# A graph layer on one core: the scan, the moved VectorE steps and the edge look-up of its first two parts rewritten

## The chip, the cores and the metric

The kernel runs on one core of one Trainium2 chip. The metric is the device time of one execution in microseconds (us). TensorE is called PE in the profile, its weight load PEld, VectorE is DVE, ScalarE is ACT, GpSimd is POOL and SyncE is SP. Each engine works through its own queue of instructions in the order in which they were built into the program.

## The reference

The layer has 6250 nodes with 256 features and 206,250 edges, each a pair (src, dst). A node is normalised to `xn`. Three things are then computed and added.

```
h  = xn @ W                          # 64 features a node
el = h @ Wl.T ; er = h @ Wr.T        # 4 heads a node
e  = exp(leaky_relu(el[src] + er[dst], 0.2))
w  = e / max(segment_sum(e, src), 1e-12)[src]
gnn = elu(segment_sum(w[:, head] * h[dst], src) + b)      # 4 heads x 64
x1 = x + gnn + linear_attention(xn)  # keys' softmax runs over all nodes
x2 = x1 + moe(layernorm(x1))         # 8 experts, top 2, 256 -> 256 -> 256
```

## The kernel before, in words

Nodes are cut into 49 tiles of 128 rows. The kernel has three stages.

**First part.** `project` takes the nodes in groups of 4 tiles. For each tile it normalises the rows (`xn`, L310, DVE), transposes and multiplies them by one joined weight matrix (L316, L321, PE), and ACT copies the queries, the keys with values (`kv`) and the table row (`tab`, L328) out of PSUM. DVE copies the four `el` columns (L329) and keeps a running maximum of the keys (`kmax`, L335). The table goes to DRAM; the edge stage gathers from it.

Between the groups run the 51 calls of `sort_batch`, three after each group and the last twelve after all of them. A batch is 32 columns of 128 edges. DVE builds a one-hot `ob` of each edge's block of nodes (L365). PE counts each column (L371) and DVE turns the counts into running sums (the scan, L375) and subtracts the column's own count (`before`, L380). `ahead` (L390) spreads that for a matmul. PE adds the rank within the column (`tri`, L398) and `ahead` (L399). ACT copies the result to f16, and DVE multiplies by `ob` (L410), sums over the 26 blocks (L413), doubles the rank (`rank2`, L415) and compares it with a row of numbers (`ohp`, L422). PE then places the edges with it (L428). `context` runs beside the last twelve batches: it takes the maximum off the keys (L468, DVE), exponentiates (L469, ACT) and multiplies keys by values (L472, PE).

**Edge stage.** `pack(q)` makes the edge list for the two node tiles 2q and 2q+1. It counts with two matmuls (`here` L830, `total` L832) and a scan (L833), goes through `to_i` (L846 to L848) to the one-hots `ohc`, `rc` and `ohp` in seven rounds (L858, L865, L870, DVE), and sums them into `s_ps` (L875, PE). From `s_i` (L880) come the gather's indices `dst_x` (L886). Then POOL issues the gathers: 35 for each tile (L906), in five buffers `xe` of seven gathers each; eight such buffers exist. `pack(q+1)` is called in the middle of tile 2q.

For each tile `look` fetches `el` of the edges' own nodes. It builds one-hots `oh` (L919), transposes them in two halves (L932) and multiplies them with `elw` (L939). The result stands in PSUM once for each of 12 column groups, 4 quarters and 3 bf16 parts. DVE sums the three parts into `er` (L943), once for each half. At the start of the tile `weights` puts the quarters' columns in place and adds them up (L960 to L964), then adds the gathered `xe` of the five buffers one after the other (L967), and forms `z` (L969), the exponential and `bank` (L972). `sums` multiplies the one-hots by the weights (`ohw`, L980, DVE) and sums the gathered rows (`a_ps`, L987, PE).

**Between the steps of the edge stage** the function `some_more` issues the next step of other work: first `attention`, and then for each block of 4 finished node tiles `finish_steps`: `front` (L640 to L675), `route` (L692 to L723) and the experts, `hidden` (`h_ps`, L731) and `result`. `result` puts one `y_ps` (L747) for each tile and expert, which DVE adds to `x` (L751). The last experts run after the last tile.

The order on each engine is not the order of the source. A scheduler places every instruction when the program is built, by its own costs, so a change in one step can move others.

Of the kernel before, what the change touches and what calls it, by code (L numbers as in the profile page):

```python
# [35 lines left out]
def tile_gps_layer(  # L36
# [173 lines left out]

    tri = sp.tile([P, P], F16, name="tri")
    nc.vector.tensor_scalar(tri, iota_f, piota, None, op0=OP.is_gt)
    delta = sp.tile([NB, NB], F16, name="delta")
    nc.vector.tensor_scalar(delta, iota_f[:NB, :NB], piota[:NB], None, op0=OP.is_equal)

    starts = sp.tile([NB, BW // CB, CB], F32, name="starts")
    nc.vector.memset(starts, 1.0)
    nc.vector.memset(starts[:, :, 0:1], 0.0)

# [68 lines left out]
    def project(t0, n):  # L288
# [15 lines left out]
        nc.vector.tensor_scalar_mul(rn[:, :n], rn[:, :n], float(D) ** 0.5)  # L304
        tab = qw.tile([P, GT, TW], F32, name="tab")
        nc.gpsimd.memset(tab[:, :, TW - 1:TW], 1.0)  # L306
        for j in range(n):
            t = t0 + j
            xn = qw.tile([P, D], F32, name="xn")
            nc.vector.tensor_scalar(  # L310
                xn, xt[:, j, :], stats[:, t, 0:1], rstd[:, t:t + 1],
                op0=OP.subtract, op1=OP.mult,
            )
            xT_ps = mps.tile([P, DC, P], F32, name="tp")
            for c in range(DC):
                nc.tensor.transpose(xT_ps[:, c, :], xn[:, c * P:(c + 1) * P], ident)  # L316
            xT = qw.tile([P, DC, P], F32, name="xT")
            nc.scalar.copy(xT, xT_ps)
            pr = mps.tile([P, PW], F32, name="pr")
            for c in range(DC):  # L320
                nc.tensor.matmul(  # L321
                    pr, lhsT=xT[:, c, :], rhs=wcat[:, c, :], start=(c == 0), stop=(c == DC - 1)
                )
            nc.scalar.activation(q_all[:, t, :], pr[:, :HID], AF.Copy, scale=rn[:, j:j + 1])
            nc.scalar.activation(
                kv[:, t, :2 * HID], pr[:, HID:3 * HID], AF.Copy, scale=rn[:, j:j + 1]
            )
            nc.scalar.copy(tab[:, j, :TW - 1], pr[:, O_TAB:O_EL])  # L328
            nc.vector.tensor_copy(el[:, t, :], pr[:, O_EL:PW])  # L329
            rows = P if t < NT - 1 else last  # L330
            k_t = kv[:rows, t, :HID]
            if t == 0:
                nc.vector.tensor_copy(kmax, k_t)
            else:
                nc.vector.tensor_max(kmax[:rows], kmax[:rows], k_t)  # L335
        nc.sync.dma_start(
            out=table[t0 * P:(t0 + n) * P, :].rearrange("(t p) f -> p t f", p=P),
            in_=tab[:, :n, :],
        )
# [8 lines left out]
    def sort_batch(t):  # L348
# [19 lines left out]
        )  # L368
        n_ps = sps.tile([NB, BW], F32, name="n_ps")
        for c in range(w):  # L370
            nc.tensor.matmul(  # L371
                n_ps[:, c:c + 1], lhsT=ob[:, c, :], rhs=ones16[:, 0:1], start=True, stop=True
            )
        inc = sw.tile([NB, BW], F32, name="inc")
        nc.vector.tensor_tensor_scan(  # L375
            inc[:, :w], flat(starts)[:, :w], n_ps[:, :w], 0.0,
            op0=OP.mult, op1=OP.add,
        )
        before = sw.tile([NB, BW, 2], F16, name="before")
        nc.vector.tensor_tensor(  # L380
            before[:, :w], inc[:, :w, None].to_broadcast([NB, w, 2]),
            n_ps[:, :w, None].to_broadcast([NB, w, 2]), op=OP.subtract,
        )
        if w == BW:
            nc.scalar.copy(ntot[:, bs], inc[:NQ].rearrange("q (b c) -> q b c", c=CB)[:, :, CB - 1])
        else:
            for b, e in enumerate(ends):
                nc.scalar.copy(ntot[:, bs][:, b:b + 1], inc[:NQ, e - 1:e])
        ahead = sw.tile([NB, BW, NB], F16, name="ahead", bufs=1)
        nc.vector.tensor_tensor(  # L390
            pairs(ahead[:, :w]), two(before[:, :w], NB // 2), row(delta, NB // 2), op=OP.mult
        )
        r_ps = sps.tile([P, BW // BB, 512], F32, name="r_ps")
        r16 = sw.tile([P, BW, NB], F16, name="r16", bufs=1)
        for i, a in enumerate(range(0, w, BB)):
            z = min(w, a + BB)
            part = r_ps[:, i, :(z - a) * NB]
            nc.tensor.matmul(part, lhsT=tri, rhs=flat(ob[:, a:z]), start=True, stop=False)  # L398
            nc.tensor.matmul(  # L399
                part, lhsT=ones16[:NB, :], rhs=flat(ahead[:, a:z]), start=False, stop=True  # L400
            )
# [8 lines left out]
        nc.vector.tensor_tensor(flat(r16[:, :w]), flat(r16[:, :w]), flat(ob[:, :w]), op=OP.mult)  # L410
        rank = sw.tile([P, BW], F16, name="rank")
        with nc.allow_low_precision("one summand of each sum is not zero"):
            nc.vector.tensor_reduce(rank[:, :w], r16[:, :w], axis=AX.X, op=OP.add)  # L413
        rank2 = sw.tile([P, BW, 2], F16, name="rank2")
        nc.vector.tensor_copy(rank2[:, :w], rank[:, :w, None].to_broadcast([P, w, 2]))  # L415
        rv = sw.tile([P, BW, 2, NB], F16, name="rv")
# [23 lines left out]

    def context():
        km_ps = mps.tile([HID, P], F32, name="tp")
        nc.tensor.transpose(km_ps, kmax, ident)
# [371 lines left out]
    def pack(q):  # L815
# [8 lines left out]
        for u in range(U):  # L824
# [5 lines left out]
            nc.tensor.matmul(flat(here), lhsT=upto, rhs=flat(ohs), start=True, stop=True)  # L830
            total = pe.tile([P, S, NBT], F32, name="e_ps")
            nc.tensor.matmul(flat(total), lhsT=ones16, rhs=flat(ohs), start=True, stop=True)  # L832
# [82 lines left out]
    def look(b, k):  # L915

        if k == 0:
# [6 lines left out]
            )  # L924
            seen[b] = oh, gw.tile([P, GC, S, H], F32, name="er")
        elif k < 3:
            oh, er = seen[b]
            gh = GC // 2
# [14 lines left out]
            nc.vector.tensor_reduce(  # L943
                er[:, g0:g0 + gh].rearrange("p g s h -> p (g s) h"),
                e_ps.rearrange("p g s i h -> p (g s) h i"), axis=AX.X, op=OP.add,
            )

    def weights(xes, er):
        z = gw.tile([P, CW, H], F32, name="z")

        def of(q0, n, a, m):

            zq = z[:, q0 * CS:(q0 + n) * CS].rearrange("p (s j) h -> p s j h", j=CS)
            return zq[:, :, a:a + m]

        def er_of(q0, n, a, m):
            return er[:, a:a + m, q0:q0 + n].rearrange("p g s h -> p s g h")

        more = GC - 1 - CS
        nc.vector.tensor_copy(of(0, S, 0, CS), er_of(0, S, 1, CS))  # L960
        nc.vector.tensor_copy(z[:, CPT - more:CPT], er[:, GC - more:, S - 1])
        head, tail = of(1, S - 1, 0, more), of(0, S - 1, CS - 1, 1)
        nc.vector.tensor_add(head, head, er_of(0, S - 1, GC - more, more))
        nc.vector.tensor_add(tail, tail, er_of(1, S - 1, 0, 1))  # L964
        for k, xe in enumerate(xes):
            zk = z[:, k * EB:(k + 1) * EB]
            nc.vector.tensor_add(zk, zk, xe[:, :, :H])  # L967
# [210 lines left out]
```

## Time and profile before

| | |
|---|---|
| median of 17 runs | 3153.06 us (3148.53 to 3166.56) |
| profiled execution | 3159.26 us, span of its instructions 3157.5 us |
| mean granted clock of TensorE | 0.782 of full speed |
| busy: PE, PEld, DVE, ACT, POOL | 2163.7, 1642.1, 2040.3, 681.9, 1753.9 us |
| first gather starts | 492.82 us |
| gathers | 1715 (L906), mean 1016 ns |

In a timeline or chain row the first number is the start in us from the span's start and the second the length in us; a bracket holds the idle time of the engine before it and what ended it, as far as the profile could infer. In a row of a group "busy us, mean ns | idle before" follow the shapes. A row of windows gives, for one stretch of time, each engine's busy time.

### The profile page before, as it was taken

Reading aid. Unit: us, or ns where it says so; the run is one execution under the profiler, and the core shown is the slowest. Engines: PE = TensorE matmul, PEld = TensorE weight load, DVE = VectorE, ACT = ScalarE, POOL = GpSimd, SP = SyncE. Lnnn points to the kernel's source line nnn. Section 1 sums busy time; section 2 is a strip of 40 time slices with the busy share of each in tenths; the row PEclk is TensorE's granted clock in tenths of the full one; section 3 lists DMA queues with packets and bytes.
Section 4 is the critical chain, followed back from the end, with each engine's and each line's share of the span. In section 5 each row is a group of like instructions: output and inputs, shape, how many; then the busy total and the mean of one; then the engine's idle time right before and its main releaser. Section 6 shows DMA issues by size and latency. Waiting matters only on the chain. (4 is left out here: it accounts for less than half of the span.)

```text
span 3157.5 us, 40348 instructions
## 1 busy us (share of the span) xinstructions
PE 2163.7 (69%) x15298; PEld 1642.1 (52%) x15298; DVE 2040.3 (65%) x4719; ACT 681.9 (22%) x1365; POOL 1753.9 (56%) x1753
## 2 busy tenths in 40 slices
PE   6777763454545487768877778587685885848868
PEld 3444442344444365646665566456564564646645
DVE  8888886476667547655764685556755666556733
ACT  3333320111221122122222121121120211212123
POOL 1000005777777565578666575775766757757520
PEclk8777665766667688879887888688796887968879
DMA  2000201132222311121111111211112112111110
GB/s 63 27 26 20 20 1 33 24 66 53 54 51 39 89 25 33 21 41 23 36 29 33 29 33 23 40 27 29 33 26 38 27 28 33 29 30 31 28 15 9
DMA packets 106684, 103.98 MB, mean 33 GB/s; under 512 B 42726, under 2 KB 78788, under 8 KB 106484
## 3 DMA queue, kind: packets, MB, share of 16 engines
q0 software_dynamic: 54880, 60.70, 13.5%
q1 hardware_dynamic: 49908, 39.75, 4.5%
q8 instruction: 122, 2.00, 0.3%
q10 hardware_dynamic: 1696, 0.89, 0.1%
q14 instruction: 78, 0.64, 0.1%
HBM read 86.57 MB, written 14.65 MB: 32 GB/s over the span
## 5 line engine op out<-in xcount | busy, mean ns | idle before, releaser
L906 POOL DMA_INDIRECT xe<-table,dst_x x1715 | 1742.5, 1016 | 982.2 <-issue 486.5
L987 PE MATMUL a_ps<-ohw,xe 128*65 128x128 f32 x4410 | 619.5, 301 | 52.1 <-DVE ohw L980 51.9
L987 PEld LDWEIGHTS a_ps<-ohw,xe 128*65 128x65 f32 x4410 | 574.6, 156 | 95.5 <-DVE ohw L980 74.1
L747 PE MATMUL y_ps<-w2s,hT 128*128 128x256 f32 x1568 | 414.8, 406 | 105.5 <-DVE x L751 90.9
L747 PEld LDWEIGHTS y_ps<-w2s,hT 128*128 128x128 f32 x1568 | 307.4, 204 | 211.6 <-DVE x L751 103.2
L731 PE MATMUL h_ps<-tokT,w1s 128*128 128x512 f32 (+2 forms) x896 | 401.4, 565 | 7.1 <-ACT hT L739 5.7
L967 DVE TENSOR_TENSOR z<-z,xe 128x28 f32<-128x28 f32 x245 | 40.9, 188 | 551.8 <-DMA xe<-table,dst_x 537.8
L980 DVE TENSOR_TENSOR ohw<-oh,bank 128x1280 f32<-128x1280 bf16 x196 | 322.6, 1650 | 110.7 <-PE a_ps L987 109.8
L875 PE MATMUL s_ps<-rc,ohp 128*128 128x144 f16 x2525 | 240.7, 264 | 178.3 <-DVE rc L865 157.3
L751 DVE SCALAR_TENSOR_TENSOR x<-y_ps,comb,x 128x256 f32<-128x256 f32 x392 | 187.0, 481 | 240.4 <-PE y_ps L747 239.5
L875 PEld LDWEIGHTS <-ohp 128*128 128x128 f16 x2525 | 218.2, 116 | 229.0 <-issue 131.5
L739 ACT ACTIVATE hT<-h_ps,b1s 128x512 f32<-128x512 f32 (+2 forms) x224 | 141.9, 634 | 538.1 <-PE h_ps L731 477.2
L865 DVE TENSOR_TENSOR rc<-ohc,grid 128x1152 f16<-128x1152 f16 (+1 forms) x350 | 229.5, 696 | 0.0
L731 PEld LDWEIGHTS h_ps<-tokT,w1s 128*128 128x128 f32 x896 | 157.4, 198 | 107.0 <-issue 74.4
L870 DVE TENSOR_TENSOR ohp<-to,iota_h 128x2048 f16<-128x2048 f16 (+1 forms) x175 | 195.5, 1117 | 0.7 <-PE s_ps L875 0.6
L306 POOL MEMSET tab<- 128x4 f32 x13 | 1.3, 109 | 282.1 <-DMA table<-tab 255.5
L971 ACT ACTIVATE ew<-z 128x140 f32<-128x140 f32 x49 | 15.6, 319 | 645.4 <-DVE z L969 645.3
L932 PE MATMUL t_ps<-identb,oh 128*128 128x128 bf16 x588 | 64.2, 259 | 116.9 <-DVE oh L919 116.0
L832 PE MATMUL e_ps<-ohs,ones 128*128 128x404 f16 x50 | 20.2, 403 | 149.8 <-DVE er L943 141.4
L858 DVE TENSOR_TENSOR ohc<-to,iota_h 128x1152 f16<-128x1152 f16 (+1 forms) x175 | 121.6, 695 | 0.4
L428 PE MATMUL g_ps<-rv,ohp 128*128 128x52 f16 x1612 | 66.5, 205 | 77.4 <-DVE ohp L422 77.4
L422 DVE TENSOR_TENSOR ohp<-rank,iota_h 128x4096 f16<-128x4096 f16 (+1 forms) x51 | 114.9, 2252 | 0.0
(261 smaller groups left out, 2649.3 us busy)
## 6 DMA issues: line engine op xcount, KB each, us to landing
xe<-table,dst_x POOLq DMA_INDIRECT x1715
xt<-in_x_dram SPq DMA_DIRECT2D x24, 512.0 KB, 3.9
base_y<-xt SPq DMA_DIRECT2D x12, 512.0 KB, 3.0
yt<-base_y SPq DMA_DIRECT2D x11, 512.0 KB, 3.9
out_dram<-x SPq DMA_DIRECT2D x11, 512.0 KB, 3.0
w1s<-in_L_ffn_w_dram SPq DMA_DIRECT2D x8, 256.0 KB
w2s<-in_L_ffn_w_dram SPq DMA_DIRECT2D x8, 256.0 KB, 4.4
table<-tab SPq DMA_DIRECT2D x12, 138.0 KB
```

Source lines behind the costliest of these rows:

```text
L422: nc.vector.tensor_tensor(pairs(ohp[:, :w]), two(rank2[:, :w], P // 2), row(iota_h, P // 2), op=OP.is_equal)
L731: nc.tensor.matmul(h_ps[:, :w], lhsT=w1s[:, e, c, f * P:(f + 1) * P], rhs=held["tokT"][:, c, :w], start=(c == 0), stop=(c == DC - 1),)
L739: nc.scalar.activation(held[e][:, f, :w], h_ps[:, :w], AF.Gelu, bias=b1s[:, k:k + 1])
L747: nc.tensor.matmul(y_ps, lhsT=held[e][:, f, j * P:(j + 1) * P], rhs=w2s[:, e, f, :], start=(f == 0), stop=(f == FC - 1),)
L751: nc.vector.scalar_tensor_tensor(x2[:, j, :], y_ps, held["comb"][:, j, e:e + 1], x2[:, j, :], op0=OP.mult, op1=OP.add,)
L858: nc.vector.tensor_tensor(pairs(ohc[:, :m]), twos(to[:, 0, t0:t0 + m], U * CW // 2), iota_2[:, :, :U * CW // 2].to_broadcast([P, m, U * CW ...
L865: nc.vector.tensor_tensor(pairs(rc[:, :m, i, :]), pairs(ohc[:, :m]), twos(grid[:, q, t0:t0 + m, i, :], U * CW // 2), op=OP.mult,)
L870: nc.vector.tensor_tensor(pairs(ohp[:, :m]), twos(to[:, 1, t0:t0 + m], P // 2), iota_2.to_broadcast([P, m, P // 2, 2]), op=OP.is_equal,)
L875: nc.tensor.matmul(flat(s_ps), lhsT=ohp[:, t - t0, :], rhs=flat(rc[:, t - t0]), start=(t == 0), stop=(t == NBT - 1),)
L906: nc.gpsimd.indirect_dma_start(out=xe[:, j, :], out_offset=None, in_=table, in_offset=bass.IndirectOffsetOnAxis(ap=dst_x[:, c:c + 1], axis=0),
L980: nc.vector.tensor_tensor(ohw[:, :n], oh[:, g0:g1, i, None, :].to_broadcast([P, n, H, SN]), ew_s[:, c0:c0 + n, :, None].to_broadcast([P, n ...
L987: nc.tensor.matmul(a_ps[:, i].rearrange("f h n -> f (h n)"), lhsT=xes[c // EB][:, c % EB, H:], rhs=ohw[:, c - c0].rearrange("p h n -> p (h ...
```

## The change

1. `sort_batch`: the counts are made as pairs (count, 0), so that one scan over the 64 numbers gives a running sum that serves directly; `before` (L380) goes, and `ahead` and the rank are formed from the inclusive sums (`upto` takes the place of `tri`). The sum over 26 blocks becomes one addition of 12 blocks onto 12 and a sum over 14. `rank2` is made by ACT.
2. `project`: ACT makes `xn` with a scale and a bias (`shift`, one small DVE instruction for each group). ACT's copy of `tab` takes the `el` columns along and POOL copies them on for each group. The running maximum goes; `context` takes one maximum over all of `kv`. POOL takes the maximum off the keys.
3. `look` and `weights`: one matmul writes zeros over the tile's sums in PSUM, and the 12 products add to it there, each at the columns where it belongs. One DVE sum over the three parts takes the place of two sums, two copies and two additions. `total` of `pack` gets a buffer of the other PSUM pool.

```diff
-            n_ps[:, c:c + 1], lhsT=ob[:, c, :], rhs=ones16[:, 0:1]   # sort_batch
+            n_ps[:, c, :], lhsT=ob[:, c, :], rhs=one_none
-        nc.vector.tensor_tensor_scan(inc[:, :w], flat(starts)[:, :w], n_ps[:, :w], ...)
-        nc.vector.tensor_tensor(before[:, :w], inc..., n_ps..., op=OP.subtract)
+        nc.vector.tensor_tensor_scan(flat(inc[:, :w]), starts..., flat(n_ps[:, :w]), ...)
-            pairs(ahead[:, :w]), two(before[:, :w], NB // 2), row(delta, NB // 2), op=OP.mult
+            pairs(ahead[:, :w]), two(inc[:, :w], NB // 2), row(delta, NB // 2), op=OP.mult
-            nc.tensor.matmul(part, lhsT=tri, rhs=flat(ob[:, a:z]), start=True, stop=False)
+            nc.tensor.matmul(part, lhsT=upto, rhs=flat(ob[:, a:z]), start=True, stop=False)
+        nc.vector.tensor_tensor(
+            r16[:, :w, :fold], r16[:, :w, :fold], r16[:, :w, NB - fold:], op=OP.add
+        )
-            nc.vector.tensor_reduce(rank[:, :w], r16[:, :w], axis=AX.X, op=OP.add)
+            nc.vector.tensor_reduce(rank[:, :w], r16[:, :w, :NB - fold], axis=AX.X, op=OP.add)
-        nc.vector.tensor_copy(rank2[:, :w], ...)
+        nc.scalar.copy(rank2[:, :w], ...)
...
-            nc.vector.tensor_scalar(xn, xt[:, j, :], ...)                 # project
+            nc.scalar.activation(xn, xt[:, j, :], AF.Identity, bias=shift[:, j:j + 1], ...)
-            nc.vector.tensor_copy(el[:, t, :], pr[:, O_EL:PW])
-                nc.vector.tensor_max(kmax[:rows], kmax[:rows], k_t)
+        nc.gpsimd.tensor_copy(el[:, t0:t0 + n, :], tab[:, :n, TW - 1:])
+        nc.gpsimd.memset(tab[:, :n, TW - 1:TW], 1.0)
...
+        nc.vector.tensor_reduce(kmax, kv[:, :NT - 1, :HID].rearrange("p t d -> p d t"), ...)
-            nc.vector.tensor_sub(kk, kk, krow[:, None, :].to_broadcast([P, n, HID]))   # context
+            nc.gpsimd.tensor_sub(kk, kk, krow[:, None, :].to_broadcast([P, n, HID]))
...
-            total = pe.tile([P, S, NBT], F32, name="e_ps")               # pack
+            total = pt.tile([P, S, NBT], F32, name="t_ps")
...
+            if k == 1:                                                   # look
+                nc.tensor.matmul(e_ps..., lhsT=identb[0:1, :], rhs=none, start=True, stop=False)
             for g in range(gh):
                 nc.tensor.matmul(
-                    e_ps[:, g].rearrange("p s i h -> p (s i h)"), lhsT=ohT[:, g, :],
-                    rhs=elw..., start=True, stop=True,
+                    e_ps[:, g0 + g::CS][:, :S]..., lhsT=ohT[:, g, :],
+                    rhs=elw..., start=False, stop=(g0 + g == GC - 1),
                 )
-            nc.vector.tensor_reduce(er[:, g0:g0 + gh]..., e_ps..., axis=AX.X, op=OP.add)
...
-        nc.vector.tensor_copy(of(0, S, 0, CS), er_of(0, S, 1, CS))       # weights
-        nc.vector.tensor_copy(z[:, CPT - more:CPT], er[:, GC - more:, S - 1])
-        nc.vector.tensor_add(head, head, er_of(0, S - 1, GC - more, more))
-        nc.vector.tensor_add(tail, tail, er_of(1, S - 1, 0, 1))
+        nc.vector.tensor_reduce(z, e_ps[:, 1:].rearrange("p c i h -> p c h i"), ...)
         for k, xe in enumerate(xes):
             nc.vector.tensor_add(zk, zk, xe[:, :, :H])
```

More of the change, by code (lines that the diff above doesn't have):

```diff
@@ L209, in tile_gps_layer @@
     sps = sx.enter_context(tc.tile_pool(name="sortp", bufs=1, space=PSUM))
-    tri = sp.tile([P, P], F16, name="tri")
-    nc.vector.tensor_scalar(tri, iota_f, piota, None, op0=OP.is_gt)
     delta = sp.tile([NB, NB], F16, name="delta")
     nc.vector.tensor_scalar(delta, iota_f[:NB, :NB], piota[:NB], None, op0=OP.is_equal)
-    starts = sp.tile([NB, BW // CB, CB], F32, name="starts")
+    starts = sp.tile([NB, BW // CB, CB, 2], F32, name="starts")
     nc.vector.memset(starts, 1.0)
-    nc.vector.memset(starts[:, :, 0:1], 0.0)
+    nc.vector.memset(starts[:, :, 0:1, 0:1], 0.0)
+    one_none = sp.tile([P, 2], F16, name="one_none")
+    nc.vector.memset(one_none, 0.0)
+    nc.vector.memset(one_none[:, 0:1], 1.0)
     bid = sp.tile([P, EC, 2], F16, name="bid")
@@ L304, in project @@
         nc.vector.tensor_scalar_mul(rn[:, :n], rn[:, :n], float(D) ** 0.5)
-        tab = qw.tile([P, GT, TW], F32, name="tab")
-        nc.gpsimd.memset(tab[:, :, TW - 1:TW], 1.0)
+        shift = qw.tile([P, GT], F32, name="shift")
+        nc.vector.scalar_tensor_tensor(
+            shift[:, :n], stats[:, t0:t0 + n, 0], -1.0, rs, op0=OP.mult, op1=OP.mult
+        )
+        tab = qw.tile([P, GT, TW - 1 + H], F32, name="tab")
         for j in range(n):
@@ L309, in project @@
             xn = qw.tile([P, D], F32, name="xn")
-            nc.vector.tensor_scalar(
-                xn, xt[:, j, :], stats[:, t, 0:1], rstd[:, t:t + 1],
-                op0=OP.subtract, op1=OP.mult,
+            nc.scalar.activation(
+                xn, xt[:, j, :], AF.Identity, bias=shift[:, j:j + 1], scale=rstd[:, t:t + 1]
             )
@@ L327, in project @@
             )
-            nc.scalar.copy(tab[:, j, :TW - 1], pr[:, O_TAB:O_EL])
-            nc.vector.tensor_copy(el[:, t, :], pr[:, O_EL:PW])
[L330 to L334, printed above, removed]
-                nc.vector.tensor_max(kmax[:rows], kmax[:rows], k_t)
+            nc.scalar.copy(tab[:, j, :], pr[:, O_TAB:PW])
+        nc.gpsimd.tensor_copy(el[:, t0:t0 + n, :], tab[:, :n, TW - 1:])
+        nc.gpsimd.memset(tab[:, :n, TW - 1:TW], 1.0)
         nc.sync.dma_start(
             out=table[t0 * P:(t0 + n) * P, :].rearrange("(t p) f -> p t f", p=P),
-            in_=tab[:, :n, :],
+            in_=tab[:, :n, :TW],
         )
@@ L368, in sort_batch @@
         )
-        n_ps = sps.tile([NB, BW], F32, name="n_ps")
+        n_ps = sps.tile([NB, BW, 2], F32, name="n_ps")
         for c in range(w):
             nc.tensor.matmul(
-                n_ps[:, c:c + 1], lhsT=ob[:, c, :], rhs=ones16[:, 0:1], start=True, stop=True
+                n_ps[:, c, :], lhsT=ob[:, c, :], rhs=one_none, start=True, stop=True
             )
-        inc = sw.tile([NB, BW], F32, name="inc")
+        inc = sw.tile([NB, BW, 2], F16, name="inc")
         nc.vector.tensor_tensor_scan(
[L376 to L382, printed above, removed]
+            flat(inc[:, :w]), starts.rearrange("q b c two -> q (b c two)")[:, :2 * w],
+            flat(n_ps[:, :w]), 0.0, op0=OP.mult, op1=OP.add,
         )
         if w == BW:
-            nc.scalar.copy(ntot[:, bs], inc[:NQ].rearrange("q (b c) -> q b c", c=CB)[:, :, CB - 1])
+            nc.scalar.copy(
+                ntot[:, bs],
+                inc[:NQ].rearrange("q (b c) two -> q b c two", c=CB)[:, :, CB - 1, 0],
+            )
         else:
             for b, e in enumerate(ends):
-                nc.scalar.copy(ntot[:, bs][:, b:b + 1], inc[:NQ, e - 1:e])
+                nc.scalar.copy(ntot[:, bs][:, b:b + 1], inc[:NQ, e - 1, 0:1])
         ahead = sw.tile([NB, BW, NB], F16, name="ahead", bufs=1)
         nc.vector.tensor_tensor(
-            pairs(ahead[:, :w]), two(before[:, :w], NB // 2), row(delta, NB // 2), op=OP.mult
+            pairs(ahead[:, :w]), two(inc[:, :w], NB // 2), row(delta, NB // 2), op=OP.mult
         )
@@ L411, in sort_batch @@
         rank = sw.tile([P, BW], F16, name="rank")
+        fold = NB // 4 * 2
+        nc.vector.tensor_tensor(
+            r16[:, :w, :fold], r16[:, :w, :fold], r16[:, :w, NB - fold:], op=OP.add
+        )
         with nc.allow_low_precision("one summand of each sum is not zero"):
-            nc.vector.tensor_reduce(rank[:, :w], r16[:, :w], axis=AX.X, op=OP.add)
+            nc.vector.tensor_reduce(
+                rank[:, :w], r16[:, :w, :NB - fold], axis=AX.X, op=OP.add
+            )
         rank2 = sw.tile([P, BW, 2], F16, name="rank2")
-        nc.vector.tensor_copy(rank2[:, :w], rank[:, :w, None].to_broadcast([P, w, 2]))
+        nc.scalar.copy(rank2[:, :w], rank[:, :w, None].to_broadcast([P, w, 2]))
         rv = sw.tile([P, BW, 2, NB], F16, name="rv")
@@ L441, in context @@
     def context():
+        nc.vector.tensor_reduce(
+            kmax, kv[:, :NT - 1, :HID].rearrange("p t d -> p d t"), axis=AX.X, op=OP.max
+        )
+        nc.vector.tensor_max(kmax[:last], kmax[:last], kv[:last, NT - 1, :HID])
         km_ps = mps.tile([HID, P], F32, name="tp")
@@ L802, in tile_gps_layer @@
     yps = gx.enter_context(tc.tile_pool(name="yp", bufs=2, space=PSUM))
+    none = gw.tile([1, (1 + CPT) * 3 * H], BF16, name="none", bufs=1)
+    nc.vector.memset(none, 0.0)
     pv = gx.enter_context(tc.tile_pool(name="pv", bufs=1, space=PSUM))
@@ L924, in look @@
             )
-            seen[b] = oh, gw.tile([P, GC, S, H], F32, name="er")
+            seen[b] = oh, pe.tile([P, 1 + CPT, 3, H], F32, name="e_ps")
         elif k < 3:
-            oh, er = seen[b]
+            oh, e_ps = seen[b]
             gh = GC // 2
@@ L936, in look, with weights @@
             nc.scalar.copy(ohT, t_ps)
-            e_ps = pe.tile([P, gh, S, 3, H], F32, name="e_ps")
+            if k == 1:
+                nc.tensor.matmul(
+                    e_ps.rearrange("p c i h -> p (c i h)"), lhsT=identb[0:1, :], rhs=none,
+                    start=True, stop=False,
+                )
             for g in range(gh):
                 nc.tensor.matmul(
-                    e_ps[:, g].rearrange("p s i h -> p (s i h)"), lhsT=ohT[:, g, :],
-                    rhs=elw[:, b].rearrange("p s i h -> p (s i h)"), start=True, stop=True,
-                )
[L943 to L959, printed above, removed]
-        nc.vector.tensor_copy(of(0, S, 0, CS), er_of(0, S, 1, CS))
-        nc.vector.tensor_copy(z[:, CPT - more:CPT], er[:, GC - more:, S - 1])
-        head, tail = of(1, S - 1, 0, more), of(0, S - 1, CS - 1, 1)
-        nc.vector.tensor_add(head, head, er_of(0, S - 1, GC - more, more))
-        nc.vector.tensor_add(tail, tail, er_of(1, S - 1, 0, 1))
+                    e_ps[:, g0 + g::CS][:, :S].rearrange("p s i h -> p s (i h)"),
+                    lhsT=ohT[:, g, :],
+                    rhs=elw[:, b].rearrange("p s i h -> p s (i h)"),
+                    start=False, stop=(g0 + g == GC - 1),
+                )
+    def weights(xes, e_ps):
+        z = gw.tile([P, CPT, H], F32, name="z")
+        nc.vector.tensor_reduce(
+            z, e_ps[:, 1:].rearrange("p c i h -> p c h i"), axis=AX.X, op=OP.add
+        )
         for k, xe in enumerate(xes):
@@ L967, in weights @@
             nc.vector.tensor_add(zk, zk, xe[:, :, :H])
-        zz = z[:, :CPT]
-        nc.vector.scalar_tensor_tensor(zz, zz, 0.2, zz, op0=OP.mult, op1=OP.max)
+        nc.vector.scalar_tensor_tensor(z, z, 0.2, z, op0=OP.mult, op1=OP.max)
         ew = gw.tile([P, CPT, H], F32, name="ew")
-        nc.scalar.activation(ew, zz, AF.Exp)
+        nc.scalar.activation(ew, z, AF.Exp)
         nc.vector.tensor_copy(ew_s, ew)
@@ L1016, in tile_gps_layer @@
             xes, _ = ready.pop(b)
-            oh, er = seen.pop(b)
-            weights(xes, er)
+            oh, e_ps = seen.pop(b)
+            weights(xes, e_ps)
             a_ps = pa.tile([FO + 1, S, H, SN], F32, name="a_ps")
```

## The prediction, made before the changed kernel ran

> **What bounds the kernel now.** I read the page first: the chain that ended last, then the costliest groups.
>
> ```profile
> PE 13%; DVE 11%; POOL 8%; issue 4%; DMA 4%; ACT 0%; POOLq 0%; DVEq 0%; ACTq 0%
> ...
> L906 POOL DMA_INDIRECT xe<-table,dst_x x1715 | 1742.5, 1016 | 982.2 <-issue 486.5
> ...
> L967 DVE TENSOR_TENSOR z<-z,xe 128x28 f32<-128x28 f32 x245 | 40.9, 188 | 551.8 <-DMA xe<-table,dst_x 537.8
> ```
>
> No engine is the bound of the whole. POOL's gathers come nearest, and in the edge stage DVE sits idle before the gathered rows (L967) for 552 us. So the question is what POOL waits for. POOL's timeline, window by window, shows one gather every 1.25 us and real pauses only ahead of the first gather of an even tile, where new indices are needed:
>
> ```profile
> 2271.33 0.94 POOL L906 DMA_INDIRECT xe<-table,dst_x  x1 [1.70 <-issue]
> ...
> 2358.98 1.04 POOL L906 DMA_INDIRECT xe<-table,dst_x  x1 [0.30 <-issue]
> 2379.24 0.94 POOL L906 DMA_INDIRECT xe<-table,dst_x  x1 [19.21 <-PE y_ps L747]
> ```
>
> These are tiles 34 and 36 (35 gathers each). The pauses alternate, 1 to 4 us and about 19 us, once per block of four tiles, and a block takes 201.6 us (2271.33 to 2472.92). PE is named, but POOL waits for `dst_x`, which ended at 2378.49. Its way there, in DVE's timeline:
>
> ```profile
> 2317.61 0.49 DVE L967 TENSOR_TENSOR z<-z,xe 128x28 f32<-128x28 f32 x4 [9.75 <-DMA xe<-table,dst_x]
> ...
> 2347.68 0.98 DVE L833 TENSOR_TENSOR_SCAN inc<-ones,e_ps 128x404 f32<-128x404 f32 x1
> ...
> 2355.30 0.76 DVE L858 TENSOR_TENSOR ohc<-to,iota_h 128x1152 f16<-128x1152 f16 x1
> ```
>
> Tile 34's rows are there at 2317.6; 30 us of PE work, mostly experts, stand ahead of `total`; from the first `ohc` it is 23.9 us to the gather. Together 61.6 us, against 43.7 us for one tile's gathers.
>
> What the order on DVE is worth is seen once in this trace, at tile 12, in DVE's and POOL's timelines:
>
> ```profile
> 1073.28 0.19 DVE L967 TENSOR_TENSOR z<-z,xe 128x28 f32<-128x28 f32 x1 [8.37 <-DMA xe<-table,dst_x]
> ...
> 1076.83 0.75 DVE L858 TENSOR_TENSOR ohc<-to,iota_h 128x1152 f16<-128x1152 f16 x1
> ```
>
> ```profile
> 1079.28 1.29 POOL L906 DMA_INDIRECT xe<-table,dst_x  x1 [0.30 <-issue]
> 1115.66 0.94 POOL L906 DMA_INDIRECT xe<-table,dst_x  x1 [35.09 <-PE s_ps L830]
> ```
>
> There `ohc` stands behind the addition of the odd tile's fourth buffer, and behind `front` and `route`; POOL stands still for 35.1 us.
>
> The first part is DVE's. Windows, and DVE's groups from 40 to 452 us:
>
> ```profile
> core 0: us, PE busy (x) PEld busy (x) DVE busy (x) ACT busy (x) POOL busy (x), PEclk, DMA share, GB/s
> 40.00:360.00 320.00, 243.19 (x2822) 141.07 (x2820) 282.09 (x663) 110.90 (x360) 1.20 (x11) 0.74 0.14 25
> 360.00:452.00 92.00, 68.86 (x876) 51.91 (x876) 79.07 (x144) 23.90 (x63) 0.00 (x0) 0.61 0.01 1
> ```
>
> ```profile
> L413 DVE TENSOR_REDUCE rank<-r 128x32 f16<-128x832 f16 x49 | 49.2, 1003 | 0.0
> ...
> L310 DVE TENSOR_SCALAR xn<-xt,stats,rstd 128x256 f32<-128x256 f32 x44 | 17.7, 407 | 12.7 <-PE tp L316 12.1
> ```
>
> DVE is busy 361 of 412 us.
>
> **First part, DVE.** Neighbours overlap by about 0.07 us, so each instruction counts as its mean less 0.07. Removed: `before` 50 x 0.13 = 6.4; `rank2` 50 x 0.11 = 5.6; `xn` 49 x 0.34 = 16.5; `el` 49 x 0.09 = 4.4; `kmax` 48 x 0.21 = 10.2; the subtraction L468 (669 ns) 7.4. The sum over 26 (1.003 us for 832, 0.454 for 312: 1.06 ns each) becomes 0.60 us for 448, plus an addition of 384 in f16, which lies between 0.30 us (312) and 0.58 (832): 0.34; saved 0.13 x 50 = 6.7. Removed in all 57 us. Added: a scan of 64 for 32, 0.06 x 50 = 3; `shift` 1.2; the one maximum over 6144 elements, by L413's rate 6.5 us (3.3 by the f16 comparisons' 0.55 ns, 13 if the long stride doubles it). Net 46 us off DVE.
>
> On the path there is a new wait: DVE's `rank`, ACT's `rank2`, DVE's `ohp`, where L422 had no idle time. An ACT step between two DVE steps costs its length plus 0.39 us (2318.44 to 2319.15 around a 319 ns exponential), here 0.57 us; one 0.5 us `rv` mostly stands between. Free, that is 0.1 us a batch; on a busy ACT I take 0.4, 20 us. If every second `rank2` stood behind an ACT copy that waits for PE (L324 waits 1.84 us each time) it would be 56 us. So the first part gains 26 us, between 46 and -10.
>
> `xn` on ACT (467 ns by L325, 23 us) and `rank2` lie beside DVE, ACT being busy 153 of 475 us; without that cover they cost their 33 us. POOL's 13 subtractions and `el` copies have no row: the cast L235 gives 0.89 ns an element, so 0.5 us for 512; twice that with two inputs and one DVE step in the way, about 2. POOL idles 188 us before its first gather, so I take 0.5 us for the last one. SP's queue keeps its order.
>
> A rule against this move: the Trainium skill, "SBUF — State Buffer", section "Who interferes with whom", says that a DVE instruction with two SBUF inputs and a POOL instruction that reads SBUF block each other for a whole instruction. The row: gathers take 0.94 us alone and up to 1.75 beside the one-hots of `pack`. By the rule each of the 26 POOL steps could wait one `ohp` of 2.28 us, all but the last hidden; the sum moves by 2 us.
>
> **Look-up, by itself.** For each tile two `er` (454 ns), two copies and two additions (311, 154, 185, 171) become one sum of 420 elements, 0.6 us: 1.1 us less DVE. The zero matmul (nearest row `total`, 404 columns, 0.40 us) is 20 us of PE in all; PE is busy 143 of 201.6 us a block, so it costs 0, or 0.4 us a pair without that slack. `total` no longer waits for `er`.
>
> **Look-up, by the new order.** This term decides. The built program has another order on DVE. For the block of tiles 32 to 35, small steps left out:
>
> ```
> before, tile 32: bank ohw front ... to_i ohc rc ohp (7 rounds) route s_i dst_x | L967 x5 (rows of 33)
> after,  tile 32: bank ohw front | L967 x4 to_i ... L967 (fifth) | ohc ohp rc (7 rounds) route s_i dst_x
> before, tile 34: bank, 13 y additions (L751), first scan of pack
> after,  tile 34: bank, 20 y additions, first scan of pack
> ```
>
> All five additions of the odd tile's rows now stand ahead of `ohc`, so indices for tile 34 can't be made until tile 33's last gather has landed. This holds for six pairs: the packs for tiles 26, 30, 34, 38, 42 and 46. Their pauses now average 2.2 us (3.59, 2.95, 1.70, 1.70, 2.00, 1.04). After: last gather's end to its landing 2.8 (3.7 in the chain less 0.94), landing to `ohc` 1.0, `ohc` to the gather 23.9: 27.7 us. That adds 25.5. The rounds then no longer lie over gathers: 70 gathers took 92.0 us (2379.24 to 2472.92 less the pause) where 1.25 each makes 87.5; 4 us come back. **+21.5 us, six times: +129.**
>
> Behind it waits `route`, so the experts start later: 7 more y ahead of the next scan. One y with its share of `hidden` is 1.73 us of PE (8 records of `y_ps` 1.73 us for two y, 4 of `h_ps` 1.72 likewise), and that stretch has PE busy 28.2 of 29.5 us. 7 x 1.73 = 12.1, less 1 us of `er`. **+11, six times: +66** (0 to +14 each). Late next are the `xe` buffers, which the later sums release: 0 to 5 us a block, taken as 0.
>
> The other packs: for tile 12 `ohc` now stands ahead of the odd rows and only `s_i` behind them, so 35.1 becomes about 11: -24. For tile 20 (pause 14.2) all five additions come first: +13. Seven others gain the 1.1 us and an y or so, 1.5 each: -10.
>
> **Sum.** -26 + 129 + 66 - 24 + 13 - 10 = +148. On the profiled 3159.3 us that is 3307; that execution lies 6.2 us above the median, so the median goes from 3153.1 to 3301.
>
> **Rivals.**
> - *The experts keep up* (17%). If PE fills the 25 us pauses, the second term is nothing: 3301 - 66 = 3235. For: PE idles there. Against: the 20 y.
> - *Deeper* (13%). ACT holds `rank2` (+36) and the buffers cost 5 us a block (+30): 3367.
> - *Faster: the pauses merge* (7%). The 19.2 us pause exists because 61.6 us of chain stand against 43.7 of gathers. Were the experts' work done in the new pause, the second one would go: -19.2 x 6 in place of +66, 3301 - 66 - 115 = 3120. It decides from 11 fewer y (19.2 / 1.73) ahead of the scan; the order shows 7 more.
> - *The gate is none* (3%): the fifth rows come early enough that nothing waits. Then -26 - 21 alone: 3106. Against: the landing is the end of a POOL that is always at work.
>
> **Numbers.** The sum as worked out has 58%, the slower rivals 17 and 13, the faster ones 10; 2% fall between, within 0.2%, which is about what a measurement of this kernel tells from no change. The range reaches from below 3235 to above 3367: 3225 to 3375.
>
> **Right or wrong in the profile after.** First gather at about 467 us for 492.8. Pauses of 25 to 31 us ahead of tiles 26, 30, 34, 38, 42, 46 after a DVE wait for `xe`; about 30 ahead of 28, 32, 36, 40, 44, 48; 234 us a block. Gathers nearer 0.95 us. It is wrong if those six pauses stay under 10 us, or if the other six shrink.

## The result: 185 us slower, and the profile after

The changed kernel takes 3337.8 us (median of 8 runs, 3332.7 to 3347.0) against 3153.2 for the kernel before: a ratio of 1.059, 95% interval 1.057 to 1.061. The forecast was 3301 with a range of 3225 to 3375, and slower with a chance of 0.88. The profiled execution has a span of 3350.4 us, 193 more than before's 3157.5. It lies 15 us above its median where before's lay 6 above, so sums made on the two profiles come out some 9 us high.

The costliest groups of the page, in the same columns as before (busy, mean ns | idle ahead of them and its releaser):

```profile
L917 POOL DMA_INDIRECT xe<-table,dst_x x1715 | 1733.3, 1011 | 1126.8 <-issue 739.5
...
L969 DVE TENSOR_TENSOR z<-z,xe 128x28 f32<-128x28 f32 x245 | 45.4, 190 | 792.6 <-DMA xe<-table,dst_x 779.1
```

Gathering itself costs what it did. What grew is DVE's wait for gathered rows, by 241 us, and POOL's idle time, by 145. POOL's timeline at the first gather, at the first gathers of tiles 34 and 36, and at a gather inside tile 35:

```profile
459.12 3.99 POOL L917 DMA_INDIRECT xe<-table,dst_x  x1 [96.72 <-issue]
...
2337.87 0.94 POOL L917 DMA_INDIRECT xe<-table,dst_x  x1 [25.53 <-issue]
...
2407.84 0.94 POOL L917 DMA_INDIRECT xe<-table,dst_x  x1 [8.29 <-DVE x L760]
...
2460.97 0.94 POOL L917 DMA_INDIRECT xe<-table,dst_x  x1 [26.92 <-PE y_ps L756]
```

Before, these pauses were 1.7 and 19.2 us, and nothing stopped inside tile 35. Both kinds of pause have grown. DVE's timeline shows the reason of the first: `ohc` of the pack for tile 34 stands right behind the fifth addition of tile 33's rows, which waited for its gather.

```profile
2314.62 0.19 DVE L969 TENSOR_TENSOR z<-z,xe 128x28 f32<-128x28 f32 x1 [2.55 <-DMA xe<-table,dst_x]
2315.20 0.75 DVE L869 TENSOR_TENSOR ohc<-to,iota_h 128x1152 f16<-128x1152 f16 x1
...
2336.94 0.19 DVE L897 TENSOR_SCALAR dst_x<-dst_x 128x72 int32<-128x72 int32 x1
```

And of the second, the path to tile 36: the even tile's last addition, the first scan of `pack`, its first `ohc`.

```profile
2384.85 0.23 DVE L969 TENSOR_TENSOR z<-z,xe 128x28 f32<-128x28 f32 x1 [4.65 <-DMA xe<-table,dst_x]
...
2428.21 1.00 DVE L844 TENSOR_TENSOR_SCAN inc<-ones,t_ps 128x404 f32<-128x404 f32 x1 [0.24 <-PE t_ps L843]
...
2435.80 0.76 DVE L869 TENSOR_TENSOR ohc<-to,iota_h 128x1152 f16<-128x1152 f16 x1
```

From addition to scan it is 43.4 us, where it was 30.1 (2317.61 to 2347.68). The 193 us by the starts of the gathers: first gather 33.7 earlier; tiles 0 to 24 longer by 2.7; the six pairs of tiles that end in the first kind of pause, called gated here (24 to 26, 28 to 30, ..., 44 to 46), longer by 134.7; the six others (26 to 28, ..., 46 to 48) by 87.8; from tile 48 to the end by 1.4.

### The profile page after: what moved, and what is told of

It is laid out like the page before. It is cut to its first block, busy times and chain, and to the rows that moved or that the text cites. A ratio compares the mean times of both kernels' runs of the same rounds, so it can differ in the third digit from the quotient of the medians.

```text
span 3350.4 us, 40258 instructions
## 1 busy us (share of the span) xinstructions
PE 2207.4 (66%) x15347; PEld 1639.3 (49%) x15347; DVE 1974.7 (59%) x4280; ACT 710.5 (21%) x1464; POOL 1781.5 (53%) x1779
## 3 DMA queue, kind: packets, MB, share of 16 engines
q0 software_dynamic: 54880, 60.70, 12.8%
## 5 line engine op out<-in xcount | busy, mean ns | idle before, releaser
L988 PE MATMUL a_ps<-ohw,xe 128*65 128x128 f32 x4410 | 597.1, 295 | 53.7 <-DVE ohw L981 51.4
L988 PEld LDWEIGHTS a_ps<-ohw,xe 128*65 128x65 f32 x4410 | 553.3, 152 | 131.3 <-DVE ohw L981 112.3
L756 PE MATMUL y_ps<-w2s,hT 128*128 128x256 f32 x1568 | 435.3, 418 | 163.0 <-DVE x L760 69.6
L756 PEld LDWEIGHTS y_ps<-w2s,hT 128*128 128x128 f32 x1568 | 318.3, 211 | 283.0 <-issue 81.5
L740 PE MATMUL h_ps<-tokT,w1s 128*128 128x512 f32 (+2 forms) x896 | 424.5, 595 | 3.8 <-ACT hT L748 2.8
L740 PEld LDWEIGHTS h_ps<-tokT,w1s 128*128 128x128 f32 x896 | 167.2, 207 | 112.4 <-issue 85.8
L333 POOL COPY el<-tab 128x16 f32<-128x16 f32 (+1 forms) x13 | 14.8, 1141 | 271.4 <-ACT tab L332 271.4
L675 PE MATMUL y_ps<-ident,tok 128*128 128x128 f32 x98 | 30.7, 411 | 173.2 <-DVE tok L669 172.4
L947 ACT COPY ohT<-t_ps 128x768 bf16<-128x768 bf16 x98 | 78.1, 797 | 247.3 <-PE t_ps L943 246.8
L325 PE MATMUL pr<-wcat,xT 128*128 128x456 f32 x196 | 109.8, 689 | 4.9 <-ACT xT L322 4.1
```

The costliest lines, as they stand in the source:

```text
L740: nc.tensor.matmul(h_ps[:, :w], lhsT=w1s[:, e, c, f * P:(f + 1) * P], rhs=held["tokT"][:, c, :w], start=(c == 0), stop=(c == DC - 1),)
L756: nc.tensor.matmul(y_ps, lhsT=held[e][:, f, j * P:(j + 1) * P], rhs=w2s[:, e, f, :], start=(f == 0), stop=(f == FC - 1),)
L988: nc.tensor.matmul(a_ps[:, i].rearrange("f h n -> f (h n)"), lhsT=xes[c // EB][:, c % EB, H:], rhs=ohw[:, c - c0].rearrange("p h n -> p (h ...
```

## The experiments

Theory A: the order on DVE costs the time, since it puts gathered rows ahead of the work that makes the next indices. Theory B: the new look-up is slow by itself (sums in PSUM in strides, a matmul of zeros, a long-held buffer). Theory C: the moves to ACT and POOL cost time. Pauses are read in POOL's timeline.

**The first two parts without the third.**

```diff
 # sort_batch, project and context as in the changed kernel; pack, look and weights as before
-            total = pt.tile([P, S, NBT], F32, name="t_ps")
+            total = pe.tile([P, S, NBT], F32, name="e_ps")
-        nc.vector.tensor_reduce(z, e_ps[:, 1:].rearrange("p c i h -> p c h i"), ...)
+        # the er sums, two copies and two additions of the kernel before
```

> The change without its third part: the scan, rank2, xn, el and kmax of the changed kernel, with the old look-up (four er sums, total in the bank of e_ps). Theory A, the order on DVE in the edge stage is what costs time, and that order comes from the look-up's part: the pauses ahead of tiles 26, 30, ... stay at 1 to 4 us and those ahead of 28, 32, ... at 18 to 20 as in the kernel before, the first gather stands at about 459 us as in the changed kernel, and the time is 3153 - 34 = 3119 (3105 to 3130). Theory C, the moves to ACT and POOL cost something in the edge stage (the slower el copies, kmax, ACT): 3153 or more in spite of the earlier first gather.

Measured: 3102.0 us, ratio 0.983 (0.980 to 0.986): 52 us faster than before. Its POOL timeline at the first gather and at tiles 34 and 36:

```profile
451.13 3.40 POOL L915 DMA_INDIRECT xe<-table,dst_x  x1 [96.67 <-issue]
...
2214.04 0.95 POOL L915 DMA_INDIRECT xe<-table,dst_x  x1 [0.45 <-issue]
...
2322.21 0.95 POOL L915 DMA_INDIRECT xe<-table,dst_x  x1 [19.21 <-PE y_ps L756]
```

From tile 24 on the pauses are those of the kernel before, so C falls: the lighter first part is a gain, of 42 us at the first gather and of 14 between there and tile 24. It is faster than the 3105 to 3130 expected.

**The third part alone.**

```diff
 # the kernel before, with look, weights and total of the changed kernel
-            total = pe.tile([P, S, NBT], F32, name="e_ps")
+            total = pt.tile([P, S, NBT], F32, name="t_ps")
-        nc.vector.tensor_copy(of(0, S, 0, CS), er_of(0, S, 1, CS))   # and the rest of the old sum
+        nc.vector.tensor_reduce(z, e_ps[:, 1:].rearrange("p c i h -> p c h i"), ...)
```

> The kernel before with the third part alone (new look-up, one sum over its parts, total in a buffer of its own). Theory A and theory B (the new look-up is itself slow: sums in PSUM in strides, the zero matmul, a PSUM buffer held until the sum): 3153 + 185 + 34 = 3372 (3355 to 3385), first gather at 493 us as before, six pauses of 25 to 30 us ahead of tiles 26, 30, ..., 46. Theory C (the moves to ACT and POOL cost the time): 3150 to 3170 and pauses of 1 to 4 us there.

Measured: 3383.2 us, ratio 1.073 (1.069 to 1.077). The parts add up: +229 and -52 make +177 beside the +185 of the whole. The same three places:

```profile
494.62 2.42 POOL L908 DMA_INDIRECT xe<-table,dst_x  x1 [189.23 <-DVE loc L896]
...
2374.84 0.94 POOL L908 DMA_INDIRECT xe<-table,dst_x  x1 [25.53 <-issue]
...
2497.88 0.94 POOL L908 DMA_INDIRECT xe<-table,dst_x  x1 [26.92 <-PE y_ps L747]
```

These are the pauses of the changed kernel, behind the first part of the old one. The whole loss lies in the third part; A and B remain.

**Only the buffer of `total`.**

```diff
 # the kernel before
-            total = pe.tile([P, S, NBT], F32, name="e_ps")
+            total = pt.tile([P, S, NBT], F32, name="t_ps")
```

> The kernel before with one line of the third part: total in the PSUM buffer of its own; the look-up stays the old one. It asks which half of the third part brings the order that costs 229 us. If the one sum in PSUM and over its parts (seen by the run of the whole third part): 3153 within 10, pauses of 1 to 4 us ahead of tiles 26, 30, ... and 18 to 20 ahead of 28, 32, .... If the buffer of total: over 3300.

Measured: 3164.1 us, ratio 1.002 (1.000 to 1.004), 1 us above the range expected. POOL at tiles 34 and 36:

```profile
2281.87 0.94 POOL L906 DMA_INDIRECT xe<-table,dst_x  x1 [0.30 <-issue]
...
2389.22 0.94 POOL L906 DMA_INDIRECT xe<-table,dst_x  x1 [18.08 <-PE y_ps L747]
```

Its pauses are 0.3 to 3.3 us ahead of tiles 26, 30, ..., 46 and 18.1 ahead of 28, 32, ..., 44. So the buffer alone does not bring the bad order; the new `look` and `weights`, the sum in PSUM, are needed for it. Whether they bring it alone or only together with the buffer, no run tells.

**A fence: odd tiles' additions behind the pack.** The arithmetic is that of the changed kernel; only the order of issue is prescribed.

```diff
-        nc.vector.tensor_scalar_min(dst_x, dst_x, NPAD - 1)
+        pack_end[q] = nc.vector.tensor_scalar_min(dst_x, dst_x, NPAD - 1)
...
+        end = pack_end.get((b + 1) // U) if b % U else None
+        with tc.issue_after(end.ins) if end is not None else ExitStack():
             for k, xe in enumerate(xes):
                 nc.vector.tensor_add(zk, zk, xe[:, :, :H])
```

> The changed kernel with one thing in its order put back: the five additions of an odd tile's gathered rows are issued on DVE behind dst_x of the pack in flight, as in the kernel before for most tiles. Nothing is computed otherwise. Theory A: the pauses ahead of tiles 26, 30, ..., 46 are back at 2 to 4 us and that of tile 20 near 14; the contention of the rounds with the gathers is back (4 us each); the second pauses (27 us) stay, since 19 y still stand ahead of the next scan: 3338 - 6 x 24 + 6 x 4 - 15 = 3203 (3165 to 3225). If the experts' lateness goes with it, 3120. Theory B (the new look-up is slow whatever the order): over 3300.

Measured: 3200.4 us, ratio 1.015 (1.012 to 1.018), close to the 3203 that A worked out. POOL at tiles 34, 35 and 36:

```profile
2254.01 0.95 POOL L917 DMA_INDIRECT xe<-table,dst_x  x1 [1.59 <-issue]
...
2310.34 0.95 POOL L917 DMA_INDIRECT xe<-table,dst_x  x1 [12.83 <-PE a_ps L992]
...
2374.14 0.94 POOL L917 DMA_INDIRECT xe<-table,dst_x  x1 [17.91 <-PE y_ps L1036]
```

The gate is gone with the new look-up still in place, so B falls as its cause. 34 to 36 stays at 120.1 us (123.1 in the changed kernel, 107.9 before), since the y still stand ahead of the scan. The second pause itself came back to 17.9, which was not expected; 12.8 us of standing still inside the pair took its place. Where POOL stops within the pair is a matter of buffers; how long the pair lasts is set by the path to the next `dst_x`.

**A second pin: rows behind the experts.** As the fence, and each tile's additions also stand behind the last y that the preceding tile's turn holds.

```diff
+        more = last_more.get(b - 1)
+        with ExitStack() as order:
+            for ins in (end, more):
+                if ins is not None:
+                    order.enter_context(tc.issue_after(ins))
...
                 some_more()
+            last_more[b] = last_dve()
```

> As fence, and besides each tile's additions of gathered rows are issued behind the last y addition that the preceding tile's turn holds, so that the packs for tiles 28, 32, ... stand on DVE ahead of the even tile's rows and few y ahead of the scans. Theory A: both kinds of pause shrink to under 10 us, a block of four tiles comes to 180 to 190 us in place of 239, and the time is 2880 to 3000. Theory B: no better than fence. A third outcome, PE or the xe buffers become the bound: pauses gone ahead of even tiles but stalls inside the tiles, 3000 to 3150.

Measured: 2920.9 us, ratio 0.925 (0.922 to 0.928): 417 us less than the changed kernel with the same arithmetic, so B falls altogether. POOL at tiles 34 and 36, then DVE in the same stretch:

```profile
2104.20 1.70 POOL L917 DMA_INDIRECT xe<-table,dst_x  x1 [2.93 <-issue]
...
2199.95 0.94 POOL L917 DMA_INDIRECT xe<-table,dst_x  x1 [0.30 <-issue]
```

```profile
2135.00 0.75 DVE L869 TENSOR_TENSOR ohc<-to,iota_h 128x1152 f16<-128x1152 f16 x1
...
2160.99 0.52 DVE L981 TENSOR_TENSOR z<-z,xe 128x28 f32<-128x28 f32 x2
2161.68 0.52 DVE L981 TENSOR_TENSOR z<-z,xe 128x28 f32<-128x28 f32 x2
...
2188.41 0.19 DVE L897 TENSOR_SCALAR dst_x<-dst_x 128x72 int32<-128x72 int32 x1
```

The first `ohc` of the pack for tile 36 now begins 65 us ahead of that tile's first gather, and the additions of tile 34's rows, which have landed by then, lie between its rounds without a wait. A block takes 191.2 us (2104.20 to 2295.39; 180 to 190 were expected), the pauses of the steady blocks are under 5 us, and POOL itself is next: 70 gathers at 1.25 us are 87.5 of each pair's 95.5.

**One pin alone** (no fence):

```diff
-        end = pack_end[(b + 1) // U].ins if b % U and (b + 1) // U in pack_end else None
+        end = None
```

> The changed kernel with one pin alone: each tile's additions of gathered rows are issued behind the last y addition that the preceding tile's turn holds; no fence behind dst_x. The order on DVE comes out as in the kernel with both pins (packs for 26, 30, ... begin at the additions of tile 25, 29, ...; those for 28, 32, ... one tile earlier). Theory A: 2910 to 2935, as with both. If the fence does work of its own: over 2950.

Measured: 2928.6 us, ratio 0.926 (0.922 to 0.930). The one pin does it all.

**The pins with the old look-up**, with `total` in its own buffer and in that of `e_ps`:

```diff
 # the pinned kernel, with er, two copies and two additions in place of the one sum; in the second:
-            total = pt.tile([P, S, NBT], F32, name="t_ps")
+            total = pe.tile([P, S, NBT], F32, name="e_ps")
```

> The pinned kernel with the old look-up (two er sums, two copies and two additions a tile) but with total in its own PSUM buffer as in the changed kernel. On DVE the order is nearly that of the pinned kernel: packs for tiles 28, 32, ... begin before the even tile's rows. It asks what the new look-up is worth when order is out of the way. Theory A (only order matters; POOL's gathers are the bound now): 2921 + 0 to 40 = 2921 to 2960, pairs of tiles 95 to 97 us. Theory D (the new sum saves its 1.1 us of DVE and more in each tile on the path): 2960 to 3000. Theory B (the new look-up costs time of its own): under 2900.

> The pinned kernel with the old look-up and with total in the buffer of e_ps, as in the kernel before. The same pins, but total can't be written before the er sums of that buffer are done: 12 y stand ahead of the next scan, as in the kernel before. Theory A (order is what matters, and the buffer of total decides the order of the second pack): as without pins, 3085 to 3115, pauses of 17 to 20 us ahead of tiles 28, 32, .... Rival (the pins themselves give the gain, the buffer nothing): 2921 to 2960.

Measured: 2945.9 us, ratio 0.932 (0.928 to 0.937), and 2940.9 us, 0.930 (0.926 to 0.935). The second expectation was wrong under A, because it had the order of that kernel wrong: in its trace, too, the packs begin early, and the pauses ahead of tiles 28, 32, ... are 0.3 us. The rival there held: the pins carry the gain, the buffer nothing. With the order out of the way the new look-up is worth 20 to 25 us by the medians beside the kernel with both pins, and 12 to 17 beside that with one pin, which was measured together with these two. The intervals overlap, so no gain of the new look-up is shown.

**The pins on the kernel before.** No part of the change.

```diff
 # the kernel before, with pack_end, last_more and both issue_after as in the pinned kernel
```

> The kernel before, no part of the change in it, with both pins: each tile's additions of gathered rows issued behind the last y addition that the preceding tile's turn holds, and odd tiles' behind dst_x of the pack in flight. It asks whether the order alone carries the gain of the pinned kernels. Theory A (order alone): the pinned kernel with old look-up and old total, 2941, plus the first part's 42 to 51 us that it then lacks, 2983 to 2992 (2970 to 3010), first gather at 493 us, pairs of tiles 95 to 97 us. Rival (the gain needs a part of the change): 3100 or more.

Measured: 2996.4 us, ratio 0.952 (0.947 to 0.957). POOL at the first gather and at tiles 34 and 36:

```profile
491.15 3.02 POOL L906 DMA_INDIRECT xe<-table,dst_x  x1 [187.40 <-DVE loc L894]
...
2162.13 1.70 POOL L906 DMA_INDIRECT xe<-table,dst_x  x1 [2.02 <-issue]
...
2261.51 0.95 POOL L906 DMA_INDIRECT xe<-table,dst_x  x1 [0.30 <-issue]
```

Pairs take 95 to 100 us, a little more than the 95 to 97 expected. The order alone is worth 155 us of the 3151.0 measured beside it.

**`rank2` back on DVE**, in the kernel with the first two parts:

```diff
-        nc.scalar.copy(rank2[:, :w], rank[:, :w, None].to_broadcast([P, w, 2]))
+        nc.vector.tensor_copy(rank2[:, :w], rank[:, :w, None].to_broadcast([P, w, 2]))
```

> The first two parts of the change (old look-up), with rank2 back on DVE; all else as in the run of those two parts, 3102. It asks for the price of DVE's wait for rank2 on ACT, which the prediction put at 0.4 us a batch, 20 us, against 5.6 us of DVE saved. By the prediction's term: 3102 - 14 = 3088 and a first gather at 437 us. By the trace, where DVE waits for it only 2.9 us in all: 3102 + 3 = 3105, first gather at 452 to 457 us.

Measured: 3106.7 us, ratio 0.984 (0.980 to 0.988), where the kernel with `rank2` on ACT has 0.983 (0.980 to 0.986); first gather at 457.2 us. With `rank2` on ACT and the same edge stage or a pinned one it comes at 451.1 to 457.2 in six profiles (451.1 to 452.9 in five of them). The prediction's price for the wait would put it at 437 us, and no profile comes near that; whether the move is worth anything at all is below what these runs resolve.

## Why the prediction was right, by its steps

By the medians +148 was forecast and +184.6 came, so 3338 lies inside the range. On the profiles +192.9 came, and the 44.9 between are 7.7 less (first part), 5.7 more (gate), 21.8 (y), 23.7 (other packs) and 1.4 (end). Only the first part's error went against the others, so the hit owes little to errors that cancel. Of the signs named beforehand, the first gather came at 459.1 us (467), a block took 239.2 (234), the second pauses are 26.9 (about 30), and the gathers of tiles 24 to 47 took 0.96 us on average for 0.99.

**What bounds the kernel, and the gate: right.** The six pauses were forecast at 27.7 us and are 34.1, 27.1, 25.5, 27.1, 26.6 and 27.0; the term of +129 came out at +134.7. Of the 4 us that the gathers should get back, 2.9 came (36 to 38 without its pause: 89.1 us, against 92.0).

**Seven more y: right in kind, a third too small.** +66 was forecast, +87.8 came. For 34 to 36: landing 0.7 us later (47.0 into the pair for 46.3), addition to scan 13.3 longer, `ohc` to gather 1.2 longer (25.2 for 23.9), 15.2 in all for the 11 forecast. On DVE 20 y stand between addition and scan where 13 stood, as read off the built program. The window of that stretch and PE's two costliest groups in it, before and after:

```profile
2317.61:2347.68 30.07, 28.79 (x150) 21.91 (x151) 14.78 (x28) 7.10 (x10) 22.57 (x24) 0.91 0.18 29
L747 PE MATMUL y_ps<-w2s,hT 128*128 128x256 f32 x47 | 13.3, 428 | 7.1 <-DVE x L751 7.1
L731 PE MATMUL h_ps<-tokT,w1s 128*128 128x512 f32 x20 | 9.5, 596 | 0.0
```

```profile
2384.85:2428.21 43.36, 42.65 (x181) 29.47 (x182) 17.82 (x31) 9.17 (x13) 26.57 (x29) 0.92 0.15 23
L740 PE MATMUL h_ps<-tokT,w1s 128*128 128x512 f32 x39 | 20.4, 642 | 0.0
L756 PE MATMUL y_ps<-w2s,hT 128*128 128x256 f32 x76 | 19.6, 400 | 3.6 <-DVE x L795 3.6
```

The undersized term is PE's work ahead of the scan: 7 x 1.73 less 1 us for `er` was taken, 13.3 came, and PE's busy time rose by 13.9. The price of one y held (in a steady run two of them take 3.44 us, 2399.42 to 2402.86), and so did the clock, 0.92 for 0.91. But there are 19 more records of `h_ps`, 9.5 shares and not 7, against 18 fewer of `a_ps`. Nothing came off for `er`. PE also starts slowly behind its wait in both kernels: four records of `h_ps` take 3.62 us in the changed one, where four take 1.88 later, and eight of `y_ps` take 3.78 us in the one before, where eight take 1.89 later. The `xe` buffers, taken as 0, do stop POOL for 7 to 8 us inside the odd tiles, but off the path: the chain to `dst_x` explains all 15.2 us.

**The first part: right in sign, too cautious.** -26 was forecast; -33.7 in this profile, -36 to -42 in six profiles of kernels with the same first part and another order or look-up behind it. The term that failed is DVE's wait for `rank2`, 20 us. Waits and groups of DVE between 40 and 452 us:

```profile
DVE ohp L427 <- ACT rank L420: 2.9, 2, 2.4
```

```profile
L416 DVE TENSOR_REDUCE rank<-r 128x32 f16<-128x448 f16 (+1 forms) x50 | 29.6, 593 | 0.0
...
L447 DVE TENSOR_REDUCE kmax<-kv 128x128 f32<-128x6144 f32 x1 | 11.1, 11051 | 0.0
```

DVE waited for it twice, 2.9 us in all: the `rv` between covers the trip over ACT. Put 2.9 for 20 and 11.1 for the 6.5 of `kmax` (its upper end was 13), and the sum is -38. Apart from `rank2` it counts busy time and leaves out DVE's other waits, which changed both ways: 23 us of them went with `xn`, `el` and `kmax`, while the wait for ACT's copy of `r` grew by 10. The groups of `r`, before and after, in the same window:

```profile
L410 DVE TENSOR_TENSOR r<-r,ob 128x832 f16<-128x832 f16 (+1 forms) x50 | 28.7, 575 | 4.2 <-ACT r L404 4.0
```

```profile
L409 DVE TENSOR_TENSOR r<-r,ob 128x832 f16<-128x832 f16 (+1 forms) x50 | 30.4, 608 | 14.4 <-ACT r L403 14.4
```

So ACT's new work may not have been free. What makes up the 5 us from -38 to -33.7 stays open. The sum over 14 blocks, 0.593 us, was sized right. POOL's subtractions took 1.72 us on average (21.9 for 13), within the 2 allowed for each, and the last one ended at 362.4 us, 96.7 ahead of the first gather.

**The other packs: wrong by 24 us.** -21 was forecast for tiles 0 to 24, +2.7 came. The pair ahead of tile 12 gained 14.9 instead of 24 (its pause 35.1 became 15.5, not 11), that ahead of 20 lost 12.3 (13 forecast). The other ten pairs, seven of them meant to gain 10, lost 5.3 together: 6 to 8 is longer by 9.8 and 22 to 24 by 7.3. The first holds one gather of 20.75 us, told below. In the second the scan comes 7.5 us later into the pair (85.7 for 78.2), behind 12 y as before, and the pause ahead of tile 24 is 24.2 for 17.8; the third part alone has that pause too (24.0). Why the scan is late there was not found.

**The rivals.** *The experts keep up* fell, since the second term came, and larger than forecast. PE was not idle in the new pause, though; in the 25.5 us ahead of tile 34 it was busy 19.1:

```profile
2312.34:2337.87 25.53, 19.14 (x126) 11.43 (x126) 23.25 (x56) 6.71 (x11) 0.00 (x1) 0.92 0.02 2
```

It ran the rounds' sums and 20 records of `h_ps`, but no y of an expert, and the 20 y behind the pause stayed. *Deeper* fell in its mechanism (no hold by `rank2`, buffers off the path); the time lies 29 us below its 3367, by other terms. *The pauses merge* did not happen in this order. But its idea holds: once order lets the packs run ahead, in the pinned kernels, both kinds of pause shrink to a few us in the steady blocks. *The gate is none* fell with the first pause.

## What to carry to other kernels

Look at where a shorter instruction stream puts the next wait: six instructions for one is a gain only if no step that waits for data comes to stand ahead of the steps that request the next data. Count, on each in-order engine, what stands ahead of the instruction that issues the next transfers, and pin that order where a scheduler is free to change it. The price of a pause is read off the chain from landing to the next request, not off where the waiting engine happens to stop.

## What was not expected of the hardware

A gather that starts while DVE runs the one-hots of `pack` back to back sometimes lasts as long as the whole run of them. POOL's timeline and DVE's in the changed kernel:

```profile
826.18 0.94 POOL L917 DMA_INDIRECT xe<-table,dst_x  x1 [0.31 <-issue]
827.43 20.75 POOL L917 DMA_INDIRECT xe<-table,dst_x  x1 [0.30 <-DMA xe<-table,dst_x]
848.49 0.95 POOL L917 DMA_INDIRECT xe<-table,dst_x  x1 [0.30 <-issue]
```

```profile
827.27 0.75 DVE L869 TENSOR_TENSOR ohc<-to,iota_h 128x1152 f16<-128x1152 f16 x1
827.94 1.22 DVE L881 TENSOR_TENSOR ohp<-to,iota_h 128x2048 f16<-128x2048 f16 x1
829.07 1.42 DVE L876 TENSOR_TENSOR rc<-ohc,grid 128x1152 f16<-128x1152 f16 x2
...
846.77 0.60 DVE L876 TENSOR_TENSOR rc<-ohc,grid 128x360 f16<-128x360 f16 x2
```

The gather begins 0.2 us behind the first `ohc` and ends 0.8 us behind the last `rc`; the same rounds elsewhere let two gathers through in 3.1 us, of 1.50 and 1.03 us (before, 865 to 882 us). Ten of the twelve profiles, old look-up or new, have one to three gathers of 16 to 22 us: one in the kernel before (18.59 us at 1418.9), two in the changed one, three in the one with only the buffer of `total`. The pinned kernel of the best time and the one with one pin have none of that length, but each has one of 12.8 us. So the trace of before showed it already, where the prediction's row stopped at 1.75. What decides it was not found. The prediction weighed the Trainium skill, "SBUF — State Buffer", section "Who interferes with whom", by which such a pair blocks for one instruction; here the gather lasted over 28 of them. Whether it is that block, repeated, no run tells.

Longer pauses go with a lower PE clock. Four tiles, 914 matmul records each, in windows of the changed kernel and of the pinned one (length, busy time of PE, PEld, DVE, ACT, POOL, PE clock granted, DMA share, GB/s):

```profile
2337.87:2577.08 239.21, 149.89 (x914) 114.30 (x914) 122.23 (x266) 35.10 (x54) 134.94 (x140) 0.77 0.16 26
```

```profile
2104.20:2295.39 191.19, 140.36 (x914) 107.31 (x914) 121.93 (x266) 37.56 (x56) 145.55 (x141) 0.83 0.20 32
```

As many matmuls are 9.5 us of PE busy time less at 0.83 than at 0.77. Over the whole span the clock is 0.77 in the changed kernel, 0.78 before and 0.80 in the pinned one. That the waits cause it was not tested.

The one maximum cost more for each element than the sums for `rank`: `kmax` over 128 x 6144, f32 along a long stride, took 11.05 us, 1.8 ns an element, and those sums, f16 over 14 neighbours, took 1.3 (593 ns for 448). No run tells the stride from the type.
